# A hashed-attention and gated feed-forward block on one core: LayerNorm's factor in single columns on ScalarE, and another opening

## Chip, core and metric

The kernel runs on one core of a Trainium2 chip. The metric is the device time of one launch in microseconds (us). TensorE is called PE, VectorE DVE, ScalarE ACT, GpSimd POOL, and SyncE SP; SP's instructions are nearly all DMA issues.

## What is computed

The input x is 16 batches of 512 rows of 128 numbers. Each batch goes through attention over 16 heads of 8 numbers and then through a feed-forward net with ternary weights, both with LayerNorm before and after and a residual sum.

```python
def attn(x):                                  # x is already layer-normed
    q = (x @ Wq.T + bq).reshape(B, S, H, Dh)  # B 16, S 512, H 16, Dh 8
    v = (x @ Wv.T + bv).reshape(B, S, H, Dh)
    # six hash bits per row and head from q and hyperplanes: a bucket
    scores = einsum('bshd,bthd->bhst', q, q) / sqrt(128)
    coeff = 62 + (bucket[s] == bucket[t])
    return softmax(scores * coeff) @ v
def ffn(x):                                   # lin(x, w, s) = (x @ w.T) * s
    h = silu(lin(x, w1, s1)) * lin(x, w2, s2)            # 128 -> 512
    h = gelu(lin(h, h1, sh1)); h = gelu(lin(h, h2, sh2)) # 512 -> 512, twice
    return lin(h, w3, s3)                                # 512 -> 128
x = x + ln(attn(ln(x)));  x = x + ln(ffn(ln(x)))
```

`ln` subtracts the mean of a row and divides by the root of its variance plus 1e-5.

## The kernel before, in words

**One head.** A head's 512 x 512 scores are four tiles of 128 x 512. q is split into three bfloat16 parts, written to DRAM (`qd`, L619 and L620) and read back per head as two stacked operands `ql` (L779) and `qr` (L792); `bb` (L805) is the head's row of buckets, spread over all partitions. PE makes a score tile `sp` with one bfloat16 product (L827). DVE makes the coefficient tile `co` (L845: equal buckets, plus 62) and multiplies it with the scores into the logits `l`, taking the row maxima into `mxpad` in the same instruction (L874). The row maxima of two heads (`MH`) are turned by DVE (`mt`, L903), written to DRAM (`md`, L908) and read back once per head, spread over all partitions (`mb`, L920). Because the scores are symmetric, the maximum of a row can be subtracted along the free dimension: POOL subtracts `mb` from a whole head (L927), ACT takes the exponential (L932), and PE multiplies with v (`av`, L953), four heads into one bank, eight instructions for each of four steps. DVE divides (L984, L985).

**One batch.** `prep` normalizes x (the sums of later batches are made in `inputs`, in three groups), turns it on PE (L482), makes q (`qp`, L603), then on ACT q in float32 (`qs`, L625) and the first bfloat16 part (L708), on DVE and ACT the two others (L714, L718, L723), the bits (`pp`, L635, and L647) and buckets (L657 to L678), and v (`vp`, L741). `residual` norms the attention's result, adds x, and norms again (`norm_transposed`); `ffn` runs two gated products (`w`, L1066; silu at L1052), two hidden layers (`hp`, L1100; gelu at L1113) and the last product (`yp`, L1132), norms, adds and writes out. A float32 product with 512 columns is two PE instructions in the profile.

**LayerNorm.** `moments` (L378) leaves mean and variance of four row groups in columns. ACT adds epsilon (`ve`, L439), POOL raises to the power -1/2 (`rs`, L443), and DVE makes `nm` = -mean x rs in four instructions of one column each (`negate`, L448). `rescale` on ACT (L466) uses nm as bias and rs as scale. The letter after the underscore tells which: a for the input of batch 0, o for the attention's result, f for the net's input, y for its result.

**Weights.** `weights` (L1166) loads the five matrices and their scales, spread over all partitions, from SP's queue (L1185, L1186); POOL multiplies the scales into all five (L1189). h2 and w3 wait until the third head is gathered (`LATER`). The nets wait for all (`loaded`).

**What sets the order.** The order of instructions on every engine is fixed when the kernel is built. `Order` is a small planner: each step is a generator that asks for buffers (`get`), events (`wait`) or a turn on an engine with a cost in us and a rank; when an engine is free, the ready step with the lowest rank is emitted. On ACT the rank is a due time: the time at which the step became ready plus its rank, plus `SWITCH` if it needs another activation table. DMAs are steps of SP; the planner adds each DMA's size to one queue that drains at `DMA_RATE` = 160 KB per us (L180), and a step that holds for its data goes on `DMA_LAT` = 2.6 us after the queue has drained past it. On the chip each engine then executes its list strictly in this order and waits where data are not there. Score and net products share PE: scores have rank 0, attention products 1, preparation 2, the net 4. Buffers bound how far engines run ahead: 11 logit tiles (`LB`), 4 sets of gathered rows, 3 `mb`, 2 `mxpad`, 8 PSUM banks (3 for scores, 3 for the net, 2 for the rest).

Of the kernel before, what the change touches and what calls it, by code (L numbers as in the profile page):

```python
# [21 lines left out]
P = 128  # L22
# [24 lines left out]
class Order:  # L47
# [62 lines left out]
    def _step(self, p, value):  # L110
        while True:
            self.current = p
            try:
                want = p.gen.send(value)
            except StopIteration:
                self.live -= 1
                return
            value = None
            if want[0] == "get":
                pool = want[1]  # L120
                if not pool.free:
                    pool.waiters.append(p)
                    return
                value, deps = pool.free.pop(0)
                self._merge(p, deps)
            elif want[0] == "wait":
                if want[1].deps is None:
                    want[1].waiters.append(p)
                    return
                self._merge(p, want[1].deps)  # L130
            else:
                eng = want[1]
                when = max(
                    [self.now] + [
                        t + (self.LAT if e != eng else 0.0 if e in ("PE", "SP") else self.OWN)
                        for e, t in p.deps.items()
                    ]
                )
                self._at(when, self._offer, p, want, when)
                return  # L140
# [47 lines left out]
def tile_lsh_attention_ffn(  # L188
# [35 lines left out]
    ROOT = float(np.float32(E**-0.5))  # L224
    GROUPS = (1, 2, 6, B)
    LATE = 20
    EARLY, LATER = 2, 3
    SCALE = 1.0 / math.sqrt(E)
    AHEAD = 1
    MH = 2  # L230
# [41 lines left out]
    nc.gpsimd.memset(eps3, EPS / E**3)  # L272

    junk = const.tile([P, E], BF16, name="junk")
    warm = const.tile([P, 1], F32, name="warm")
    nc.scalar.activation(warm, eps, AF.Exp)

# [68 lines left out]
    def wait(event):  # L346
        return ("wait", event)
# [30 lines left out]
    def moments(src, name, rank, copy=None):  # L378
# [64 lines left out]
        yield pool(1.0, 0, lambda: nc.gpsimd.tensor_tensor(rs, ve, mhalf[:, 0], op=ALU.pow))  # L443

        def negate():

            for t in range(NT):
                nc.vector.tensor_scalar(  # L448
                    nm[:, t : t + 1],
                    mean[:, t : t + 1],  # L450
                    sign,
                    rs[:, t : t + 1],
                    op0=ALU.mult,
                    op1=ALU.mult,
                )

        yield dve(0.28, rank, negate)
        return nm, rs

    def rescale(src, dst, scales):  # L460
# [114 lines left out]
    def prep(b):  # L575
# [46 lines left out]
            yield dma(256, 1, emit, cost=0.7)  # L622
            od.set(kept[i])

        yield act(0.65, -2, lambda: nc.scalar.activation(qs, qp, AF.Identity, bias=bq_sb))  # L625
        read = Event()

        def buckets():
            yield wait(read)
# [73 lines left out]

        wrote, columned = Event(), Event()
        od.spawn(buckets())
        od.set(read)
        yield act(
            0.65, -2, lambda: nc.scalar.activation(qparts[0], qp, AF.Identity, bias=bq_sb)  # L708
        )
        od.spawn(keep(0))  # L710
        yield dve(
            0.63,
            1,
# [54 lines left out]
    def gather(j, tag):  # L768
        b, h = divmod(j, H)
        yield wait(prepared[b])  # L770
        ql = p1.tile([KS, S], BF16, tag=f"ql{tag}", name=f"ql_{j}")
        qr = p1.tile([KS, S], BF16, tag=f"qr{tag}", name=f"qr_{j}")
        bb = p1.tile([P, BR * BP], BF16, tag=f"bb{tag}", name=f"bb_{j}")
        rows[j] = (ql, qr, bb, tag)

        yield dma(
            74,
            1 + j * 1e-3,
            lambda: nc.sync.dma_start(  # L779
                out=ql,  # L780
                in_=qds[b][1][h]
                .rearrange("i d s -> (i d) s")
                .unsqueeze(1)
                .to_broadcast([NP * DH, NP, S]),
            ),
            held=False,
            cost=0.75,
        )
        yield dma(
            74,  # L790
            1 + j * 1e-3,
            lambda: nc.sync.dma_start(  # L792
                out=qr,
                in_=qds[b][0][h]
                .rearrange("d j s -> (d j) s")
                .unsqueeze(0)
                .to_broadcast([NP, NP * DH, S]),
            ),
            held=False,
            cost=0.72,  # L800
        )
# [57 lines left out]
    def logits():  # L859
        for j in range(B * H):  # L860
            kl = yield get(logit_bufs)
            if j % MH == 0:
                km, pair = (yield get(mx_bufs)), []
                mx = mxpads[int(km[2:])]
            l = p1.tile([P, NT, S], F32, tag=kl, name=f"l_{j}")
            base = j % MH * NT
            for t in range(NT):
                i = j * NT + t
                yield wait(scored[i])
                yield wait(weighed[i])  # L870
# [13 lines left out]

                yield dve(0.61, 5, emit)
                od.put(score_banks, ks)
                od.put(co_bufs, kc)
                if t < NT - 1:
                    od.loose()
            od.put(row_bufs, rows.pop(j)[3])  # L890
            ls[j] = (l, kl)
            pair.append((j, l))
            if len(pair) == MH:
                od.spawn(maxima(pair, mx, km))
            if j % GH == GH - 1:
                od.spawn(attend(j // GH))
            od.loose()
# [123 lines left out]
    def ffn(b, x1, k1, xnt, kx):  # L1021
        if b:
            yield wait(stages[b - 1][AHEAD])
        yield wait(loaded)
        kh = yield get(h_bufs)
        h = p1.tile([P, NC, S], F32, tag=kh, name=f"h_{b}_0")
        there = events(NC)
# [14 lines left out]
        def silus(c0, gates, half, held):  # L1042
# [5 lines left out]
            ]  # L1048

            def emit():  # L1050
                for a, (_, gp) in zip(tiles, gates):
# [32 lines left out]
        for layer in (1, 2):  # L1084
# [5 lines left out]
            for c0 in range(0, NC, 2):  # L1090
# [16 lines left out]
                        )  # L1107
                    got.append((c, kb, hp))

                def gelus(got=got, h=h, there=there):  # L1110
# [54 lines left out]

    def weights():  # L1166

        kl = yield get(logit_bufs)
        scales = p1.tile([P, NT, S], F32, tag=kl, name="scales")
        scale3 = const.tile([P, E], F32, name="scale3")  # L1170
        folded = []
        for i, (src, scale, nk, n, name) in enumerate((
            (w1_t, w1_s, 1, HID, "w1"),
            (w2_t, w2_s, 1, HID, "w2"),
            (h1_t, h1_s, NC, HID, "h1"),
            (h2_t, h2_s, NC, HID, "h2"),
            (w3_t, w3_s, NC, E, "w3"),
        )):
            w_sb[name] = w = const.tile([P, nk, n], F32, name=name)
            sc = scales[:, i, 0:n] if i < NT else scale3  # L1180
            folded.append(Event())

            def fetch(w=w, sc=sc, src=src, scale=scale, nk=nk):
                for i in range(nk):
                    nc.sync.dma_start(out=w[:, i, :], in_=src[i * P : (i + 1) * P, :])  # L1185
                nc.sync.dma_start(out=sc, in_=scale.partition_broadcast(P))  # L1186

            def fold(w=w, sc=sc, nk=nk, n=n):
                nc.gpsimd.tensor_tensor(  # L1189
                    w, w, sc.unsqueeze(1).to_broadcast([P, nk, n]), op=ALU.mult  # L1190
                )

            def piece(fetch=fetch, fold=fold, nk=nk, n=n, done=folded[-1], i=i):
                if i > EARLY:
                    yield wait(gathered[LATER])
                yield dma(nk * n / 2 + n / 2, 3, fetch, cost=0.42 * (nk + 1))
                yield pool(nk * n / 450, 2, fold)
                od.set(done)

            od.spawn(piece())  # L1200
        for e in folded:
            yield wait(e)
        od.put(logit_bufs, kl)
        od.set(loaded)

    with tc.manual_schedule():
        for piece in (prep(0), gathers(), scores(), coeffs(), logits(), weights(), inputs()):
            od.spawn(piece)
        od.run()

# [51 lines left out]
```

## Time and profile before

| | |
|---|---|
| time, median of 3 runs | 1388.59 us (1387.49, 1388.59, 1397.21) |
| profiled execution, its own time | 1398.15 us |
| its span | 1396.3 us |
| mean granted PE clock | 0.947 |
| busy PE, DVE, ACT, POOL | 1287.3, 1235.2, 1110.4, 1227.3 us |
| POOL's subtractions (L927) | 256, 4552 ns each, 1156.3 us |
| logits (L874), coefficients (L845) on DVE | 1024 each, 666.2 and 454.9 us |
| net's hidden products (L1100) on PE | 1024 instructions, 495.5 us |
| ACT: exponentials (L932), table loads | 256, 486.5 us; 176, 1283 ns each |
| DVE's `nm` (L448), groups o, f, y | 64 each, 9.2 us each |

Busy time of a group is the time that at least one of its instructions ran, so overlapping instructions count once. A line of a group reads: line, engine, operation, output <- inputs, shapes, count | busy us, mean ns of one | idle time of the engine in front of them, and what ended it. In the timeline view a line is the start in us, the length in us, the engine (SPq and ACTq are the queues that issue DMAs), and the same names; in brackets stands the idle time ahead of it. The page's slices cut the span into 40 parts of 34.9 us, with the busy share of each in tenths, and under PEclk the share of full clock that PE was granted.

### The profile page before, as it was taken

Reading aid. Unit: us, or ns where it says so; the run is one execution under the profiler, and the core shown is the slowest. Engines: PE = TensorE matmul, PEld = TensorE weight load, DVE = VectorE, ACT = ScalarE, POOL = GpSimd, SP = SyncE. Lnnn points to the kernel's source line nnn. Section 1 sums busy time; section 2 is a strip of 40 time slices with the busy share of each in tenths; the row PEclk is TensorE's granted clock in tenths of the full one; section 3 lists DMA queues with packets and bytes.
Section 4 is the critical chain, followed back from the end, with each engine's and each line's share of the span. In section 5 each row is a group of like instructions: output and inputs, shape, how many; then the busy total and the mean of one; then the engine's idle time right before and its main releaser. Section 6 shows DMA issues by size and latency. Waiting matters only on the chain.

```text
span 1396.3 us, 20309 instructions
## 1 busy us (share of the span) xinstructions
PE 1287.3 (92%) x5520; PEld 521.9 (37%) x5520; DVE 1235.2 (88%) x3985; ACT 1110.4 (80%) x1608; POOL 1227.3 (88%) x322
## 2 busy tenths in 40 slices
PE   4677699899899999999999999999999999999997
PEld 1111133434344343433444334434343344433353
DVE  5978899899899999999999999999999999999220
ACT  3566789889879888988989888888888897878752
POOL 2699799989999998999999999998999899999700
PEclk9666699899999999999999999999999999999999
DMA  5655355455445445444445544454544544444100
GB/s 172 188 132 157 103 149 149 120 144 140 122 112 151 119 131 144 123 142 120 148 122 133 148 122 140 128 136 127 142 126 132 136 135 134 127 112 116 46 8 8
DMA packets 158418, 176.09 MB, mean 126 GB/s; under 512 B 32480, under 2 KB 115680, under 8 KB 158304
## 3 DMA queue, kind: packets, MB, share of 16 engines
q1 hardware_dynamic: 157872, 174.59, 45.6%
q8 instruction: 44, 0.72, 0.2%
q14 instruction: 70, 0.57, 0.2%
q10 hardware_dynamic: 432, 0.20, 0.0%
HBM read 155.59 MB, written 19.14 MB: 125 GB/s over the span
## 4 chain that ended last, share of the span: by engine, by line
PE 63%; DVE 21%; issue 6%; DMA 4%; POOL 3%; ACT 2%; SPq 0%; POOLq 0%; DVEq 0%
PE hp L1100 24%; PE av L953 16%; PE sp L827 12%; DVE l L874 10%; DVE co L845 7%; PE w L1066 3%; PE yp L1132 3%; POOL l L927 2%; DMA mb<-md 2%; PE op L974 1%; PE pp L635 1%; PE qp L603 1%; DMA ql<-qd 1%; PE vp L741 1%; ACT l L932 1%
## 5 line engine op out<-in xcount | busy, mean ns | idle before, releaser
L927 POOL TENSOR_TENSOR l<-l,mb 128x2048 f32<-128x2048 f32 x256 | 1156.3, 4552 | 36.4 <-DMA mb<-md 32.0
L874 DVE CUSTOM_DVE_ANT_0 l<-co,sp 128x512 f32<-128x512 bf16 x1024 | 666.2, 686 | 29.2 <-PE av L953 22.3
L932 ACT ACTIVATE l<-l 128x2048 f32<-128x2048 f32 x256 | 486.5, 1907 | 41.2 <-POOL l L927 40.0
L1100 PE MATMUL hp<-h,h 128*128 128x512 f32 x1024 | 495.5, 596 | 0.2 <-ACT h L1113 0.2
L845 DVE TENSOR_SCALAR co<-bb,bj 128x516 bf16<-128x516 bf16 x1024 | 454.9, 477 | 3.9 <-DMA bb<-bkd 3.8
L827 PE MATMUL sp<-qr,ql 72*128 72x512 bf16 x1024 | 378.3, 404 | 80.6 <-DVE mxpad L874 68.3
L953 PE MATMUL av<-l,vaug 128*32 128x512 f32 x2048 | 280.7, 636 | 0.4 <-DVE y L1156 0.2
L1100 PEld LDWEIGHTS hp<-h,h 128*128 128x128 f32 x1024 | 190.5, 190 | 176.0 <-issue 152.9
L827 PEld LDWEIGHTS <-ql 72*128 72x128 bf16 x1024 | 96.7, 99 | 410.6 <-issue 383.4
L1066 PE MATMUL w<-xnt_f,w 128*128 128x512 f32 x256 | 133.0, 616 | 3.2 <-ACT y L390 2.0
L932 ACT ACT_TABLE_LOAD x86 | 110.3, 1283 | 1.5
L967 ACT COPY avs<-av 128x512 f32<-128x512 f32 x64 | 37.3, 582 | 90.1 <-PE av L953 90.1
L1113 ACT ACTIVATE h<-hp 128x512 f32<-128x512 f32 x128 | 71.0, 595 | 33.9 <-PE hp L1100 33.3
L953 PEld LDWEIGHTS av<-l,vaug 128*32 128x32 f32 x2048 | 47.8, 112 | 123.0 <-issue 89.9
L874 DVE DVE_READ_ACCUMULATOR2_ANT mxpad<- 128x1 f32 x1024 | 91.6, 89 | 0.0
L1113 ACT ACT_TABLE_LOAD x58 | 74.4, 1283 | 0.8
L1132 PEld LDWEIGHTS yp<-w,h 128*128 128x128 f32 x512 | 67.0, 196 | 12.7 <-issue 8.1
L1036 DVE TENSOR_TENSOR h<-w,a 128x512 f32<-128x512 f32 x64 | 43.9, 687 | 27.8 <-PE w L1066 22.0
L1132 PE MATMUL yp<-w,h 128*128 128x128 f32 x512 | 67.9, 280 | 0.0
L1066 PEld LDWEIGHTS w<-xnt_f,w 128*128 128x128 f32 x256 | 47.6, 196 | 50.9 <-issue 21.5
L443 POOL TENSOR_TENSOR rs_y<-ve_y,mhalf 128x4 f32<-128x4 f32 x16 | 16.2, 1010 | 51.8 <-issue 34.7
L448 DVE TENSOR_SCALAR nm_y<-su_y,rs_y 128x1 f32<-128x1 f32 x64 | 9.2, 210 | 38.5 <-POOL rs_y L443 38.5
(91 smaller groups left out, 868.8 us busy)
## 6 DMA issues: line engine op xcount, KB each, us to landing
mb<-md SPq DMA_DIRECT2D x256, 256.0 KB
bb<-bkd SPq DMA_DIRECT2D x256, 130.5 KB
ql<-qd SPq DMA_DIRECT2D x256, 72.0 KB
qr<-qd SPq DMA_DIRECT2D x256, 72.0 KB
qd<-q SPq DMA_DIRECT2D x96, 128.0 KB
xta<-in_L_attn_x_dram SPq DMA_DIRECT2D x16, 256.0 KB
xtr<-in_L_attn_x_dram SPq DMA_DIRECT2D x16, 256.0 KB
out_dram<-y SPq DMA_DIRECT2D x16, 256.0 KB
```

What stands on the lines that cost most here:

```text
L827: nc.tensor.matmul(sp, lhsT=ql[:, ts(t, P)], rhs=qr, start=True, stop=True)
L845: nc.vector.tensor_scalar(co, bb.rearrange("p (r c) -> p r c", c=BP)[:, :, 0:BC], bjs[b][:, c : c + 1], float(NBKT - 2), op0=ALU.is_equal, ...
L874: nc.vector.tensor_tensor_reduce(out=l, in0=co[:, 0:S], in1=sp, scale=1.0, scalar=-3.0e38, op0=ALU.mult, op1=ALU.max, accum_out=mx[:, t : ...
L927: lambda: nc.gpsimd.tensor_tensor(l, l, mb.unsqueeze(1).to_broadcast([P, NT, S]), op=ALU.subtract),
L932: yield act(1.82, 0, lambda: nc.scalar.activation(l, l, AF.Exp, scale=SCALE), "exp")
L953: nc.tensor.matmul(av[k * Q : (k + 1) * Q, :], lhsT=va[:, t, c : c + Q], rhs=ls[gg * GH + k][0][:, t, :], start=(t == 0), stop=(t == NT - 1),)
L967: yield act(0.5, -2, lambda: nc.scalar.copy(avs, av))
L1036: lambda: nc.vector.tensor_tensor(h[:, c, :], g2, a, op=ALU.mult),
L1066: lambda: nc.tensor.matmul(gp, lhsT=w_sb[which][:, 0, ts(c, P)], rhs=xnt, start=True, stop=True),
L1100: lambda i=i: nc.tensor.matmul(hp, lhsT=w[:, i, ts(c, P)], rhs=hin[:, i, :], start=(i == 0), stop=(i == NC - 1),),
L1113: nc.scalar.activation(h[:, c, :], hp, AF.Gelu)
L1132: nc.tensor.matmul(yp[:, ts(t, E)], lhsT=h[:, i, ts(t, P)], rhs=w_sb["w3"][:, i, :], start=(i == 0), stop=(i == NC - 1),)
```

## The change

`negate` moves to ACT: `mm` = sign x mean is made ahead of the power, and four ACT copies of one column each multiply it with rs. The scales of w1, h1 and h2 are no longer multiplied into the weights but given as per-partition scale columns to the silu and gelu activations; those of w2 and w3 still are. The weights are issued from ACT's queue as ACT steps with rank `LATE` (20), one after another, w2 and w3 first, h2 after the first head is gathered; only three small scale columns go by SP. PE gets `activity`, products of a zero tile (128 x 512, bfloat16) with rank 99, planned at 0.45 us each up to 10 us and at 0.25 us afterwards, until the first net is `started`. For batch 0, `qs` is made by DVE beside ACT's first part. The first head's `qr` is issued from ACT's queue. The maxima of the first four heads (`SINGLES`) are sent head by head.

```diff
@@ Order._step
+            elif want[0] == "rest":
+                self._at(self.now + want[1], self._step, p, None)
+                return
@@
-    EARLY, LATER = 2, 3
+    COLD = 10.0
+    SINGLES = 4
@@
+    still = const.tile([P, P], BF16, name="still")
+    nc.vector.memset(still, 0.0)
+    started = []
@@ moments
+        mm = p2.tile([P, NT], F32, tag=f"mm{q}", name=f"mm_{name}")
+
+        def negate():
+            for t in range(NT):
+                nc.scalar.activation(
+                    nm[:, t : t + 1], mm[:, t : t + 1], AF.Copy, scale=rs[:, t : t + 1]
+                )
+
+        yield act(0.22, -5, lambda: nc.scalar.activation(mm, mean, AF.Copy, scale=sign))
         yield pool(1.0, 0, lambda: nc.gpsimd.tensor_tensor(rs, ve, mhalf[:, 0], op=ALU.pow))
-
-        def negate():
-
-            for t in range(NT):
-                nc.vector.tensor_scalar(
-                    nm[:, t : t + 1],
-                    mean[:, t : t + 1],
-                    sign,
-                    rs[:, t : t + 1],
-                    op0=ALU.mult,
-                    op1=ALU.mult,
-                )
-
-        yield dve(0.28, rank, negate)
+        yield act(0.8, -4, negate)
@@ prep
-        yield act(0.65, -2, lambda: nc.scalar.activation(qs, qp, AF.Identity, bias=bq_sb))
         read = Event()
+
+        def copied():
+            yield dve(
+                0.66,
+                1,
+                lambda: nc.vector.tensor_scalar(qs, qp, bq_sb, None, op0=ALU.add),
+            )
+            od.set(read)
@@
-        od.set(read)
+        if b:
+            yield act(0.65, -2, lambda: nc.scalar.activation(qs, qp, AF.Identity, bias=bq_sb))
+            od.set(read)
+        else:
+            od.spawn(copied())
         yield act(
             0.65, -2, lambda: nc.scalar.activation(qparts[0], qp, AF.Identity, bias=bq_sb)
         )
         od.spawn(keep(0))
+        yield wait(read)
@@ gather
+        queue = nc.sync if j else nc.scalar
...
-            lambda: nc.sync.dma_start(
+            lambda: queue.dma_start(
                 out=qr,
...
-            cost=0.72,
+            cost=0.72 if j else 0.05,
@@ logits
-            if j % MH == 0:
+            if j < SINGLES or j % MH == 0:
                 km, pair = (yield get(mx_bufs)), []
...
-            base = j % MH * NT
+            base = len(pair) * NT
...
-            if len(pair) == MH:
+            if j < SINGLES or len(pair) == MH:
                 od.spawn(maxima(pair, mx, km))
@@ ffn
         yield wait(loaded)
+        started.append(b)
...
-                    nc.scalar.activation(a, gp, AF.Silu)
+                    nc.scalar.activation(a, gp, AF.Silu, scale=w_sb["w1s"][:, c : c + 1])
...
-                            nc.scalar.activation(h[:, c, :], hp, AF.Gelu)
+                            nc.scalar.activation(
+                                h[:, c, :], hp, AF.Gelu, scale=sc[:, c : c + 1]
+                            )
@@ weights (new body)
+        for layer, (src, scale, nk, n, name) in enumerate((
+            (w2_t, w2_s, 1, HID, "w2"),
+            (w3_t, w3_s, NC, E, "w3"),
             (w1_t, w1_s, 1, HID, "w1"),
             (h1_t, h1_s, NC, HID, "h1"),
             (h2_t, h2_s, NC, HID, "h2"),
         )):
             w_sb[name] = w = const.tile([P, nk, n], F32, name=name)
+            if layer == 4:
+                yield wait(gathered[0])
+            for i in range(nk):
+                yield act(
+                    0.42,
+                    LATE,
+                    lambda: nc.scalar.dma_start(out=w[:, i, :], in_=src[i * P : (i + 1) * P, :]),
+                )
+            if name in ("w2", "w3"):
...
+                yield act(
+                    0.42,
+                    LATE,
+                    lambda: nc.scalar.dma_start(out=sc, in_=scale.partition_broadcast(P)),
+                )
+                yield ("rest", 6.0)
+                yield pool(
+                    nk * n / 420,
+                    2,
+                    lambda: nc.gpsimd.tensor_tensor(
+                        w, w, sc.unsqueeze(1).to_broadcast([P, nk, n]), op=ALU.mult
+                    ),
+                )
...
+            else:
+                w_sb[name + "s"] = sc = const.tile([P, NC], F32, name=name + "s")
+                yield dma(
+                    2,
+                    2,
+                    lambda: nc.sync.dma_start(
+                        out=sc,
+                        in_=scale.rearrange("(c p) -> p c", p=P),
+                        allow_slow_non_contiguous=True,
+                    ),
+                    cost=0.6,
+                )
         od.set(loaded)
@@ new
+    def activity():
+        kb = yield get(ffn_banks)
+        bk = bank(kb, "activity")
+
+        def emit(start=False, stop=False):
+            nc.tensor.matmul(
+                bk,
+                lhsT=still,
+                rhs=still.unsqueeze(1).to_broadcast([P, NT, P]),
+                start=start,
+                stop=stop,
+            )
+
+        yield pe(0.45, 99, lambda: emit(start=True))
+        while not started:
+            yield pe(0.45 if od.now < COLD else 0.25, 99, emit)
+        yield pe(0.25, 99, lambda: emit(stop=True))
+        od.put(ffn_banks, kb)
```

`activity` is started last, beside the other generators.

More of the change, by code (lines that the diff above doesn't have):

```diff
@@ L442, in moments @@
         )
[L443 removed]
+        mm = p2.tile([P, NT], F32, tag=f"mm{q}", name=f"mm_{name}")
         def negate():
             for t in range(NT):
[L448 to L457 removed]
+                nc.scalar.activation(
+                    nm[:, t : t + 1], mm[:, t : t + 1], AF.Copy, scale=rs[:, t : t + 1]
+                )
+        yield act(0.22, -5, lambda: nc.scalar.activation(mm, mean, AF.Copy, scale=sign))
+        yield pool(1.0, 0, lambda: nc.gpsimd.tensor_tensor(rs, ve, mhalf[:, 0], op=ALU.pow))
+        yield act(0.8, -4, negate)
         return nm, rs
@@ L1050, in emit @@
             def emit():
-                for a, (_, gp) in zip(tiles, gates):
-                    nc.scalar.activation(a, gp, AF.Silu)
+                for i, (a, (_, gp)) in enumerate(zip(tiles, gates)):
+                    c = c0 + i
+                    nc.scalar.activation(a, gp, AF.Silu, scale=w_sb["w1s"][:, c : c + 1])
             yield act(1.2, 0, emit, "silu")
@@ L1108, in ffn, with gelus @@
                     got.append((c, kb, hp))
-                def gelus(got=got, h=h, there=there):
+                def gelus(got=got, h=h, there=there, sc=w_sb[f"h{layer}s"]):
                     def emit():
                         for c, _, hp in got:
-                            nc.scalar.activation(h[:, c, :], hp, AF.Gelu)
+                            nc.scalar.activation(
+                                h[:, c, :], hp, AF.Gelu, scale=sc[:, c : c + 1]
+                            )
                     yield act(1.2, 0, emit, "gelu")
@@ L1166, in weights @@
     def weights():
[L1168 to L1172, printed above, removed]
+        for layer, (src, scale, nk, n, name) in enumerate((
+            (w2_t, w2_s, 1, HID, "w2"),
+            (w3_t, w3_s, NC, E, "w3"),
             (w1_t, w1_s, 1, HID, "w1"),
-            (w2_t, w2_s, 1, HID, "w2"),
             (h1_t, h1_s, NC, HID, "h1"),
@@ L1176, in weights @@
             (h2_t, h2_s, NC, HID, "h2"),
-            (w3_t, w3_s, NC, E, "w3"),
         )):
             w_sb[name] = w = const.tile([P, nk, n], F32, name=name)
[L1180 to L1186, printed above, removed]
@@ L1188, in fold @@
-            def fold(w=w, sc=sc, nk=nk, n=n):
-                nc.gpsimd.tensor_tensor(
-                    w, w, sc.unsqueeze(1).to_broadcast([P, nk, n]), op=ALU.mult
-                )
[L1193 to L1203, printed above, removed]
-        od.set(loaded)
+            if layer == 4:
[5 more added lines that the diff above has]
+                    lambda: nc.scalar.dma_start(out=w[:, i, :], in_=src[i * P : (i + 1) * P, :]),
+                )
+            if name in ("w2", "w3"):
+                if name == "w2":
+                    kl = yield get(logit_bufs)
+                    sc = p1.tile([P, NT, S], F32, tag=kl, name="scale2")[:, 0, :]
+                else:
+                    sc = const.tile([P, E], F32, name="scale3")
+                yield act(
[11 more added lines that the diff above has]
+                )
+                if name == "w2":
+                    od.put(logit_bufs, kl)
+            else:
+                w_sb[name + "s"] = sc = const.tile([P, NC], F32, name=name + "s")
[9 more added lines that the diff above has]
+                )
@@ L1206, in tile_lsh_attention_ffn @@
     with tc.manual_schedule():
-        for piece in (prep(0), gathers(), scores(), coeffs(), logits(), weights(), inputs()):
+        for piece in (prep(0), gathers(), scores(), coeffs(), logits(), weights(), inputs(), activity()):
             od.spawn(piece)
```

## The prediction

> **What bounds the kernel now.** I read the slices of the span first, then busy time by stretch, then GpSimd's instructions in order of time, then SyncE's at the opening, then the chain that ended last.
>
> Slices: GpSimd (POOL) has an empty opening, a long full stretch and an empty tail, and the granted clock is low in slices 2 to 5.
>
> ```profile
> POOL 2699799989999998999999999998999899999700
> PEclk9666699899999999999999999999999999999999
> ```
>
> Busy time by stretch (columns: length, then PE, PEld, DVE, ACT, POOL busy, then clock, DMA share, GB/s). Up to 175 us PE has half or three quarters of its clock. From 250 to 1300 us, fourteen such stretches add up to 1016 us of PE, 1008 of DVE, 1002 of POOL and 895 of ACT in 1050: three engines at 95 to 97%, ACT at 85%.
>
> ```profile
> 57.00:75.00 18.00, 11.65 (x24) 1.85 (x23) 16.68 (x52) 11.05 (x21) 18.00 (x5) 0.50 0.70 165
> 150.00:175.00 25.00, 19.14 (x60) 4.88 (x59) 20.50 (x74) 16.33 (x33) 17.97 (x6) 0.58 0.41 106
> 625.00:700.00 75.00, 73.97 (x331) 30.62 (x329) 74.00 (x240) 65.23 (x84) 71.13 (x19) 1.00 0.48 137
> ```
>
> POOL's instructions in order of time: the softmax subtraction (L927), 256 times 4.52 us, first runs at 52.37 us; the last ends at 1317.6, and 78.7 us follow. From 52 us on POOL hardly rests; one hole of 7.03 us is at 155, where the first feed-forward LayerNorm's power waits for ScalarE, and ScalarE (ve_f at 161.86) stood behind a copy that waited for the av products, 1.87 us per block of eight there and 1.00 later.
>
> ```profile
> 39.86 4.51 POOL L1189 TENSOR_TENSOR h<-h,scales 128x2048 f32<-128x2048 f32 x1 [20.93 <-DMA w<-in_L_ffn_w_w_dram]
> 52.37 35.97 POOL L927 TENSOR_TENSOR l<-l,mb 128x2048 f32<-128x2048 f32 x8 [6.78 <-DMA mb<-md]
> 162.23 1.01 POOL L443 TENSOR_TENSOR rs_f<-ve_f,mhalf 128x4 f32<-128x4 f32 x1 [7.03 <-ACT ve_f L439]
> ...
> 1308.60 9.01 POOL L927 TENSOR_TENSOR l<-l,mb 128x2048 f32<-128x2048 f32 x2
> ```
>
> SyncE's queue at the opening: the first maxima are written (md) at 34.85 and read back (mb) only at 48.10, though the transfer between is 16 KB. SP issues in order; the planner counts every SP transfer into one queue of 160 KB/us (L180), so the weights' 1.6 MB (h2, w3 and their scales) put the planned landing of md some 10 us back, and other issues in front of mb.
>
> ```profile
> 34.85 0.56 SPq L908 DMA_DIRECT2D md<-mt  x1
> 37.74 2.31 SPq L1185 DMA_DIRECT2D w<-in_L_ffn_w_w_dram  x4
> 46.34 0.56 SPq L908 DMA_DIRECT2D md<-mt  x1
> 48.10 1.09 SPq L920 DMA_DIRECT2D mb<-md  x2
> ```
>
> The chain says what holds the long stretch: PE and DVE in turn.
>
> ```profile
> PE 63%; DVE 21%; issue 6%; DMA 4%; POOL 3%; ACT 2%; SPq 0%; POOLq 0%; DVEq 0%
> ```
>
> So the time is: when the subtractions start, how fast four nearly full engines pass 256 heads, and a tail.
>
> **The change, part by part.** The profiled execution took 1398.15 us (span 1396.3, 1.85 around it), 9.56 above the median 1388.59; the runs lie near 1388 and near 1397, and no view tells me why. I work out a difference, and set it against the median.
>
> *Opening, A.* The first coefficient (L845) runs at 24.57. Four edits move it. qs goes to DVE beside q0 on ACT: one ACT instruction of 0.68 leaves the line, -0.68. qp on a warmed PE: its pair took 2.07, a warm pair of the same shape (hp) 1.02, -1.05. nm_a on ACT: four columns of 0.84 in front of the scaling where DVE's first was ready after 0.28, +0.6. The first qr from ACT's queue: bb is issued 0.82 earlier (20.41 to 21.23). Sum -1.9: 22.7. Head 0's last logits ended at 29.42; alone, its maxima are turned (0.21) at 29.63 - 1.9 = 27.7, where the pair's were at 33.92. md is issued 0.93 later as before, 28.65. The gap md to mb is unknown: 13.25 and 9.74 (46.34 to 56.08) with weights in the planner's queue, 3.2 (62.70 to 65.90) without. In the new plan the weights are on ACT's queue and not counted, but the first gathers are; I take 6, nearer the last row. mb lands 4.27 after its issue (48.10 to 52.37): first subtraction at 38.9, 13.4 earlier. Pairs begin again at head 4: five more heads at 4.0 of DVE and 2.4 of the second batch's preparation put head 5's last logits at 49.9, and its mb at 61.3; POOL is ready at 38.9 + 4 x 4.52 = 57.0 and waits 4.3, where it waited 0.9 before. A = -13.4 + 3.4 = **-10**; with a gap of 3.2 it is -12.8, with 9.74 -6.3, with 13.25 -2.8.
>
> What pays for this: SP loses 19 weight and scale issues (9.4 us by its rows) and gets 3 scale columns (0.6 each by hb_sb's row) and 2 more md (0.56). ACT gets 16 weight issues of 0.43 and one qr of 0.75, 7.6 us, in a queue busy 21.5 of the first 57 us; behind a qr that waits for qd stand only sums of later batches and weights. Two more transposes cost DVE 0.4. I put +1 (0 to 5) for data that now collide with the first gathers. The folds of w1, h1, h2 leave POOL (1.27 + 2 x 4.5); they lay before 52.37, so they are worth nothing in themselves, but with POOL starting at 38.9 the h2 fold at 39.86 would have cost its 4.5.
>
> The skill's page "DMA: Bandwidth & Descriptors" (Issuing engines are not separate DMA queues) speaks against expecting much here: issuing from several engines saves only issue time, since the same 16 DMA engines move the data. By it alone the move would be worth the 0.82 and the SP issues in front of mb, 2.7, not the rest; I go by the order of SP's queue, which the rows show.
>
> *Opening, B.* Zero products fill PE's planned gaps until the first feed-forward starts, one every 0.25 us by plan, a warm 512-column bf16 product (sp) taking 0.215 in a row. If they hold the clock, av's blocks before 172 us take 1.00 for 1.87 and the 7.03 hole closes: **-7**, ends 0 (clock not held) and -10 (four slow blocks of group 4, 3.5, as well). A filler in front of a real product costs at most 0.25 and is gone before the long stretch.
>
> *LayerNorm's factor, C.* 48 LayerNorms later than the opening lose four DVE instructions each: three groups of 9.2 busy us.
>
> ```profile
> L448 DVE TENSOR_SCALAR nm_f<-mv_f,rs_f 128x1 f32<-128x1 f32 x64 | 9.2, 212 | 2.8 <-POOL rs_f L443 2.8
> L439 ACT ACTIVATE ve_f<-mv_f,eps 128x4 f32<-128x4 f32 x16 | 4.7, 294 | 6.4 <-DVE mv_f L427 6.4
> L625 ACT ACTIVATE qs<-qp,bq_sb 128x512 f32<-128x512 f32 x16 | 10.9, 680 | 7.4 <-PE qp L603 7.4
> ```
>
> Of 27.6 us, 6.9 lie on the chain (nm_f 4.31, nm_o 1.39, nm_y 1.22, added over its pieces). I take **-6.9**. Above: nothing, if PE alone sets the pace; below: -24, the part between 250 and 1300, if DVE does (PE rests 34 us there).
>
> *ACT, D.* Five small activations per LayerNorm instead. The trace has none with one column and a scale column. Bounds: 0.165 (mp, no pointer) and 0.294 (ve, bias column) each, 40 to 71 us over 48; scaling pairs show instructions of 0.485 that follow each other after 0.38, so four cost about 0.294 + 3 x 0.18 = 0.84, with mm 1.0, 48 us in all. Silu and gelu get a scale column: 0.68 (L625) against 0.595 (gelu), 192 x 0.085 = 16. ACT: +64. Cover: 155 us of ACT's rest between 250 and 1300, and only 2% of the chain is ACT's; without it all 64 show. The negation now waits for POOL's power at ACT's head, with exps and gelus behind it, where DVE stood 6.3 us up to 1310. In the tail nothing covers three LayerNorms at 0.55 more: **+1.8** with the last gelus.
>
> The skill's page "ScalarE: Activation LUTs" (Rules for kernel authors) says adds and multiplies belong on VectorE. By its figures (186 ns, 93 per pointer column, 93 of overlap; section What ACT_TABLE_LOAD costs) four columns are an estimated 0.84, DVE's four span 0.58 here: by the rule alone the move is a loss of 0.26 each, 12 us, by the chain a gain, because DVE is on it.
>
> Sum: -10 - 7 - 6.9 + 1.8 + 1 = **-21.1**. Against the profiled execution 1377.05, against the median **1367.5**.
>
> **The rivals.** *R1, DVE sets the pace.* For it: DVE at 96%, and after 57 us it rests mostly on PE. Against: PE has 63% of the chain. C is -24: 1350.4. *R2, POOL's early start is given back*: SP's order still holds mb back, or DVE falls behind. A is -3: 1374.5. *R3, ACT becomes the bound, slower.* Place: exps behind a negation that waits for POOL, so av frees logit buffers late (DVE waited 22.3 us for av already). Against: ACT rests 15%. If two thirds of its 64 us show, +42.7: 1410.2. It decides from a third (21.1 of 64); 55% make it over 1% slower. *R4, the fillers do not hold the clock*: B is 0 and qp stays cold: 1375.6.
>
> **How the numbers follow.** Forecast 0.50 (own range 1355 to 1380), R1 0.15, R2 0.15, R3 0.12, R4 0.08. 1% is 13.9 us, about what a measurement of this kernel can tell from no change: 1374.7 and 1402.5. Faster: 0.42 of the forecast, 0.15, 0.08 of R2, 0.03 of R4, 0.68. Slower: 0.09 of R3. Same: 0.23. The range goes from 1343 (R1 with A at -12.8 and B at -10 is 1344.6) to 1394 (A -3, B 0, C 0, +5 for the transfers and D's +1.8 give 1392.4), leaving out most of R3 and a little of R1, under 0.2.
>
> **What would show it.** A: the first L927 near 39 (R2: past 48), mb 3 to 10 us after the first md. B: a granted clock near 1.0 from 57 to 175, av blocks of 1.0, no 7 us hole before the first rs_f. C: no L448-like group on DVE, DVE's busy time near 1207, PE's rest from 250 to 1300 below 34. D: ACT near 1175 us busy, exps not waiting longer than now; R3 would show as DVE waiting for av far above 22 us. Wrong altogether, if the last subtraction ends less than 10 us earlier although the first starts 13 earlier.

## The result and the profile after

The changed kernel ("after") takes 1386.23 us (median of 17 runs, 1382.42 to 1390.08), the kernel before 1393.01 in its 17 runs on the same chips (1387.49 to 1397.21): a ratio of 0.995, 95% interval 0.9937 to 0.9963. It is a gain of 7 us where 21 were forecast. The profiled execution of after took 1382.42 us (span 1380.6) and is the shortest of its runs; that of before, 1398.15, is longer than all its 17. So 9 of the 15.7 us between the two traces are only the choice of execution.

The slices of after, GpSimd and the granted clock:

```profile
POOL 1599999999999999999999999989999999999200
PEclk9999999999999999999999999999999999999998
```

The low clock of slices 2 to 5 is gone, and so is GpSimd's dip to 7 in slice 5; its first two slices are no fuller than before. By stretch (length, then PE, PEld, DVE, ACT, POOL busy, clock, DMA share, GB/s), the same three stretches:

```profile
57.00:75.00 18.00, 17.97 (x89) 7.79 (x91) 17.90 (x56) 8.39 (x21) 10.63 (x4) 1.00 0.62 164
150.00:175.00 25.00, 24.87 (x131) 9.29 (x130) 23.44 (x77) 18.43 (x39) 25.00 (x8) 1.00 0.48 143
625.00:700.00 75.00, 74.68 (x344) 31.61 (x343) 73.75 (x231) 70.52 (x103) 74.73 (x20) 1.00 0.50 137
```

The clock is 1.00 for 0.50 and 0.58 (PE's busy time there now includes zero products), but from 57 to 75 us POOL is busy 10.63 of 18 us where it was busy throughout. ACT went from 65.23 to 70.52 of 75 us in the third. GpSimd's instructions in order of time:

```profile
41.17 4.53 POOL L943 TENSOR_TENSOR l<-l,mb 128x2048 f32<-128x2048 f32 x1 [20.89 <-DMA mb<-md]
48.81 9.03 POOL L943 TENSOR_TENSOR l<-l,mb 128x2048 f32<-128x2048 f32 x2 [3.11 <-DMA mb<-md]
63.82 4.53 POOL L943 TENSOR_TENSOR l<-l,mb 128x2048 f32<-128x2048 f32 x1 [5.98 <-DMA mb<-md]
69.74 22.56 POOL L943 TENSOR_TENSOR l<-l,mb 128x2048 f32<-128x2048 f32 x5 [1.39 <-DMA mb<-md]
...
159.21 1.00 POOL L459 TENSOR_TENSOR rs_f<-ve_f,mhalf 128x4 f32<-128x4 f32 x1
```

The first subtraction starts 11.2 us earlier, then POOL waits 3.11, 5.98 and 1.39 us for maxima. Its sixteenth subtraction ends at 126.7; before's ended at 127.1 (91.12 + 8 x 4.5). The hole before the first rs_f is closed. The last subtraction ends at 1283.9 for 1317.6, but 96.7 us follow for 78.7, with 128 of the nets' hidden products where before's tail had 115.

ACT's new and widened instructions, and the chain:

```profile
L1070 ACT ACTIVATE a<-w,w1s 128x512 f32<-128x512 f32 x64 | 40.9, 684 | 1.6 <-PE w L1084 0.9 <-DVE mv_o L434 0.2
L454 ACT ACTIVATE nm_y<-mm_y,rs_y 128x1 f32<-128x1 f32 x64 | 13.5, 283 | 3.0 <-POOL rs_y L459 3.0
L458 ACT ACTIVATE mm_y<-su_y 128x4 f32<-128x4 f32 x16 | 3.1, 195 | 0.0
```

```profile
PE 68%; DVE 17%; DMA 5%; ACT 4%; issue 3%; POOL 2%; SPq 1%; POOLq 0%; DVEq 0%; ACTq 0%
```

DVE lost 4 points of the chain, PE won 5, ACT rose from 2% to 4%.

### The profile page after: what moved, and what is told of

Its sections match the earlier page's. It is cut to its first block, busy times and chain, and to the rows that moved or that the text cites. A ratio compares the mean times of both kernels' runs of the same rounds, so it can differ in the third digit from the quotient of the medians.

```text
span 1380.6 us, 21164 instructions
## 1 busy us (share of the span) xinstructions
PE 1323.2 (96%) x5929; PEld 550.7 (40%) x5929; DVE 1213.3 (88%) x3793; ACT 1162.0 (84%) x1851; POOL 1217.0 (88%) x319
## 4 chain that ended last, share of the span: by engine, by line
PE 68%; DVE 17%; DMA 5%; ACT 4%; issue 3%; POOL 2%; SPq 1%; POOLq 0%; DVEq 0%; ACTq 0%
PE hp L1118 25%; PE av L969 16%; PE sp L843 13%; DVE l L890 8%; DVE co L861 5%; PE w L1084 4%; PE yp L1152 3%; PE activity L1247 3%; POOL l L943 2%; DMA mb<-md 2%; DMA bb<-bkd 1%; PE op L990 1%; ACT l L948 1%; PE vp L756 1%; DMA qr<-qd 1%
## 5 line engine op out<-in xcount | busy, mean ns | idle before, releaser
L890 DVE CUSTOM_DVE_ANT_0 l<-co,sp 128x512 f32<-128x512 bf16 x1024 | 664.6, 681 | 25.7 <-PE av L969 17.6
L861 DVE TENSOR_SCALAR co<-bb,bj 128x516 bf16<-128x516 bf16 x1024 | 449.7, 472 | 5.1 <-DMA bb<-bkd 4.9
L843 PE MATMUL sp<-qr,ql 72*128 72x512 bf16 x1024 | 356.4, 382 | 33.2 <-DVE mxpad L890 31.2
L969 PE MATMUL av<-l,vaug 128*32 128x512 f32 x2048 | 270.0, 611 | 0.0
L1247 PE MATMUL activity<-still 128*128 128x512 bf16 x409 | 109.4, 391 | 1.0 <-DVE still L280 1.0
L890 DVE DVE_READ_ACCUMULATOR2_ANT mxpad<- 128x1 f32 x1024 | 85.5, 84 | 0.0
L1247 PEld LDWEIGHTS <-still 128*128 128x128 bf16 x409 | 40.2, 100 | 58.3 <-issue 20.1
```

Source lines behind the costliest of these rows:

```text
L843: nc.tensor.matmul(sp, lhsT=ql[:, ts(t, P)], rhs=qr, start=True, stop=True)
L861: nc.vector.tensor_scalar(co, bb.rearrange("p (r c) -> p r c", c=BP)[:, :, 0:BC], bjs[b][:, c : c + 1], float(NBKT - 2), op0=ALU.is_equal, ...
L890: nc.vector.tensor_tensor_reduce(out=l, in0=co[:, 0:S], in1=sp, scale=1.0, scalar=-3.0e38, op0=ALU.mult, op1=ALU.max, accum_out=mx[:, t : ...
L969: nc.tensor.matmul(av[k * Q : (k + 1) * Q, :], lhsT=va[:, t, c : c + Q], rhs=ls[gg * GH + k][0][:, t, :], start=(t == 0), stop=(t == NT - 1),)
L1247: nc.tensor.matmul(bk, lhsT=still, rhs=still.unsqueeze(1).to_broadcast([P, NT, P]), start=start, stop=stop,)
```

## The experiments

At first I held that PE was the bound (96% busy), so that relieving DVE and adding to ACT were both worth little. Rivals: ACT's added work costs what the rest gains; the opening's gain is eaten by weight transfers. Times below are medians, with the ratio to before in brackets.

### Four undoings

**e1**: after, with the factor back on DVE.

```diff
-        yield act(0.22, -5, lambda: nc.scalar.activation(mm, mean, AF.Copy, scale=sign))
         yield pool(1.0, 0, lambda: nc.gpsimd.tensor_tensor(rs, ve, mhalf[:, 0], op=ALU.pow))
-        yield act(0.8, -4, negate)
+        yield dve(0.28, rank, negate)   # negate as in before
```

> The changed kernel with LayerNorm's factor back on DVE, all else kept (DVE +28 us of work, ACT -48). Theory PE (from the first net product on, PE's whole remaining work sets the end, and an earlier end of the attention only leaves more net products for the tail): the last subtraction ends 8 to 25 us later than the changed kernel's 1283.9, the tail is shorter by as much, and the time stays within 4 us of the changed kernel's 1386. Rival ACT (the added ACT work gave the gain back): about 20 us faster, 1366. Rival DVE (DVE sets the pace): 15 to 25 us slower, over 1400.

1371.30 us (0.9849, 0.9817 to 0.9882), nearest to the rival ACT. Giving the factor back to DVE gained 15 us on after, in this order.

**e2**: after, the weights on ACT's queue held back further.

```diff
-            if layer == 4:
-                yield wait(gathered[0])
+            if layer in (1, 3, 4):
+                yield wait(gathered[{1: 1, 3: 3, 4: 5}[layer]])
```

> The changed kernel with the loads of w3, h1 and h2 put off until the second, fourth and sixth head is gathered, so that they do not share the DMA engines with q's writes and the first gathers. Theory that these transfers cost the opening: the first coefficient comes at 23 to 24.5 us instead of 27.6, the first subtraction at 35 to 38 instead of 41.2, the first net product up to 5 us earlier than 173.4, and the time falls by what the first net product gains, 0 to 5 us. Rival (the transfers are hidden, the wait has another cause): first coefficient still past 27, time the same within 2.

1399.88 (1.0043, 1.0022 to 1.0064). The first coefficient comes at 24.76 (after 27.63), the first subtraction at 38.17 (41.17), the first product of a feed-forward net at 166.78 (173.35): so the weights do delay the opening. Yet the kernel is 14 us longer, outside theory and rival: the last subtraction ends at 1290.1 and 105 us follow.

**e3**: after without `activity()`.

```diff
-        for piece in (..., weights(), inputs(), activity()):
+        for piece in (..., weights(), inputs()):
```

> The changed kernel without the zero products. Theory PE: granted clock 0.5 to 0.8 again between 57 and 175 us, a hole of some us before the first feed-forward LayerNorm's power, first net product 3 to 10 us later than 173.4, time later by the same, 1389 to 1396. Rival (the clock of the opening is hidden behind the subtractions): time within 2 us of 1386.

1385.36 (0.9944, 0.9925 to 0.9963). Without the zero products the clock from 57 to 175 us is 0.66, where after has 1.00 (e3, then after):

```profile
57.00:175.00 118.00, 84.56 (x310) 21.46 (x310) 106.91 (x339) 75.42 (x164) 107.58 (x27) 0.66 0.52 144
57.00:175.00 118.00, 117.38 (x614) 45.43 (x613) 113.64 (x360) 77.93 (x161) 110.63 (x28) 1.00 0.54 152
```

The first net starts 9.8 us later, and the time is the same. Ten microseconds at the start were not ten at the end. But an edit also moves the planned order: DVE's sequence leaves that of after at 43 us in e2 and e3 and at 252 us in e4, so each of these three runs is one order against another.

**e4**: after, with a quarter of the second hidden layer's products left out, 55 us of PE's work.

```diff
-                    for i in range(NC):
+                    for i in range(NC if layer == 1 else NC - 1):
...
```

> The changed kernel with a quarter of the second hidden layer left out (three of four input chunks): PE loses 128 instructions of 0.43 us, 55 us, and no other engine loses anything. Theory PE: 35 to 55 us faster, 1331 to 1351, with the tail after the last subtraction shorter by most of it (97 us now). Rivals ACT and DVE: PE's work is not what sets the end, under 10 us.

1382.90 (0.993, 0.9906 to 0.9955), only 3 us below after, where my first theory said 35 to 55: PE's total work alone doesn't set the time. Stretches from the first net's start to the last subtraction's end, after and then e4:

```profile
173.35:1283.90 1110.55, 1072.93 (x4826) 442.24 (x4822) 1055.79 (x3298) 1008.96 (x1482) 1084.86 (x273) 0.99 0.48 133
```

```profile
176.27:1303.20 1126.93, 1062.24 (x4758) 432.93 (x4754) 1058.46 (x3300) 1017.10 (x1507) 1086.29 (x274) 0.97 0.47 131
```

With less to do PE rests 64.7 us instead of 37.6, at a clock of 0.97 instead of 0.99: two points of 1127 us, an estimated 23 us more. By that estimate the lost clock took nearly as much as the 27 us of longer rests. The Trainium skill's page "Perfetto Trace Analysis" (Identifying the Most-Contended Engine) takes the engine with the highest occupancy for the one to relieve first, with a caution that PE's busy share is no measure of headroom; e4 fits the caution: at 96% busy, 55 us less of PE's work took 3 us off, in this one order.

### ACT's load, and the order

e1 left two readings: ACT's added work costs time, or the hand-written planner merely fell into a luckier order. Each changed cost makes the planner choose another order for all that follows. So e5 adds work to ACT on which nothing waits, e6 does the factor's move alone, and e7 and e8 keep every instruction of after and change one planned cost by about 1% or less.

**e5**: e1 with five one-column activations per LayerNorm, written to a tile that nobody reads.

```diff
+    slack = const.tile([P, 8], F32, name="slack")
+    def ballast(src):
+        od.loose()
+        def emit():
+            for t in range(NT + 1):
+                nc.scalar.activation(slack[:, t : t + 1], eps, AF.Copy, scale=eps)
+        yield act(1.02, 3, emit)
@@ moments
+        if name[0] != "a":
+            od.spawn(ballast(src))
```

> e1 (factor on DVE) with the same five small ScalarE instructions per LayerNorm as the changed kernel's, but writing a tile that nobody reads: ACT gets the added 48 us of work, DVE keeps its factor, and nothing waits for the new instructions. Theory load (ScalarE's added work itself costs the 15 us between e1's 1371 and the changed kernel's 1386): 1383 to 1400. Rival latency (the cost is that LayerNorm's chain now passes ScalarE's queue once more): within 4 us of e1, 1367 to 1375.

**e6**: before, with the factor moved to ACT and nothing else.

> The kernel before with LayerNorm's factor on ACT alone, the opening and the scales as before. Theory that the factor on ACT costs about 15 us on either side: 1400 to 1412 against 1394 of the kernel before. The forecast's own step (6.9 us off the chain): 1385 to 1390. Rival that the cost of the factor in e1 against the changed kernel was only another order of the same instructions: anything, 1380 to 1410, without relation to 15.

**e7** and **e8**: after, in another order.

```diff
-        yield dve(0.45, 1, divide)          # e7
+        yield dve(0.455, 1, divide)
-        yield act(1.82, 0, ... AF.Exp ...)  # e8
+        yield act(1.815, 0, ... AF.Exp ...)
```

> The changed kernel with one planned cost changed, the division's, from 0.45 to 0.455 us: the same instructions, in another order. Theory order (the planner's greedy order is unstable now that four engines are nearly full, and a difference of ten microseconds between two kernels can be the order alone): 10 to 20 us faster than the changed kernel's 1386, as the planner's own clock stops 21.5 us earlier. Rival (orders differ little): 1384 to 1389.

> The changed kernel with the exponential's planned cost changed from 1.82 to 1.815 us: the same instructions, in another order. Theory order: 10 to 28 us slower than the changed kernel's 1386, as the planner's own clock stops 27.5 us later. Rival (orders differ little): 1384 to 1389.

e5 1408.33 (1.0089, 1.0056 to 1.0121), above its theory's 1400; e6 1385.65 (0.9923, 0.9898 to 0.9948); e7 1368.41 (0.9803, 0.9774 to 0.9832); e8 1415.38 (1.0136, 1.0109 to 1.0163). The same instructions in two orders differ by 47 us, seven times the result, so no single comparison of two orders says what a part of the change is worth. e5 stands 37 us above e1. Its load is this, for the whole execution (ACT's busy time grew by 42.7 us, 1127.7 to 1170.4, as small neighbours overlap):

```profile
L391 ACT ACTIVATE slack<-eps 128x1 f32<-128x1 f32 x240 | 49.2, 281 | 0.0
```

Where it shows are three waits of the loop over heads: logits that wait for a buffer which av frees (DVE l <- PE av), score products that wait for logits to leave their bank (PE sp <- DVE mxpad), subtractions that wait for maxima (POOL l <- DMA mb). The waits from 250 to 1260 us (total, times, longest), for before, after, e1, e5, e7 and e8 in turn:

```profile
POOL l L927 <- DMA mb<-md: 25.3, 15, 4.8
PE sp L827 <- DVE mxpad L874: 24.6, 54, 2.8
...
DVE l L874 <- PE av L953: 9.3, 9, 2.2
```

```profile
PE sp L843 <- DVE mxpad L890: 28.2, 59, 1.5
...
DVE l L890 <- PE av L969: 13.7, 10, 3.1
...
POOL l L943 <- DMA mb<-md: 6.7, 4, 1.9
```

```profile
PE sp L846 <- DVE mxpad L893: 18.8, 40, 2.0
...
POOL l L946 <- DMA mb<-md: 9.6, 8, 2.2
...
DVE l L893 <- PE av L972: 5.9, 3, 2.3
```

```profile
POOL l L958 <- DMA mb<-md: 32.6, 13, 8.7
PE sp L858 <- DVE mxpad L905: 29.5, 60, 1.7
DVE l L905 <- PE av L984: 21.6, 10, 4.2
```

```profile
PE sp L843 <- DVE mxpad L890: 17.4, 43, 1.5
...
DVE l L890 <- PE av L969: 6.9, 5, 2.2
POOL l L943 <- DMA mb<-md: 3.3, 2, 2.0
```

```profile
PE sp L843 <- DVE mxpad L890: 40.5, 69, 2.3
DVE l L890 <- PE av L969: 26.2, 15, 5.4
POOL l L943 <- DMA mb<-md: 21.6, 17, 3.3
```

The sums are 59, 49, 34, 84, 28 and 88 us, against profiled executions of 1398, 1382, 1370, 1406, 1364 and 1413. Over all kernels here but e4 (19) the sum and the time of the profiled execution correlate at 0.92, 0.71 us of time per us of wait, with misses up to 13 us. The waits go with the time; that they are its cause isn't shown by a correlation, and the three were picked with the traces at hand. e4 has less work than the others; its waits, 91 us, are the largest of all, and the fit would put its profiled execution at 1414 where it took 1387. So less work on PE may have been worth more than e4's 3 us, behind a poorer order. In e5 no instruction reads what the added work writes, and ACT still rests 112 us of these 1010, yet the logit buffers come back later (21.6 for 5.9). The same 1010 us in e1 and then e5:

```profile
250.00:1260.00 1010.00, 978.17 (x4434) 405.57 (x4433) 993.20 (x3206) 891.83 (x1162) 986.99 (x249) 0.99 0.48 134
250.00:1260.00 1010.00, 967.03 (x4305) 405.63 (x4303) 956.52 (x3073) 898.26 (x1327) 946.28 (x240) 0.98 0.46 130
```

### The same parts in several orders

To tell a part from an order, e9 to e14 put the edits of e7 and e8 on the other three combinations of factor and opening; e15 and e16 move a third planned cost of after by 2% either way.

```diff
e9  = e1 + divide 0.455        e10 = e1 + exp 1.815
e11 = before + divide 0.455    e12 = before + exp 1.815
e13 = e6 + divide 0.455        e14 = e6 + exp 1.815
e15 = after, avs copy 0.49 for 0.50    e16 = after, avs copy 0.51
```

> e1 (the changed kernel with the factor on DVE) in another order: the division planned at 0.455 us for 0.45, as in e7. Theory (with the factor on DVE the order is stable, and the factor on ACT costs some 15 us in the mean over orders): 1366 to 1376, near e1's 1371. Rival (e1 was a lucky order, and the factor's place is worth nothing in the mean): scattered as the changed kernel's three orders are, 1368 to 1415.

> e1 in a third order: the exponential planned at 1.815 us for 1.82, as in e8. Theory: 1366 to 1378. Rival: scattered over 1368 to 1415.

> The kernel before in another order: the division planned at 0.455 us. Theory (the kernel before has its factor on DVE too and is as stable as e1): 1388 to 1402 around its 1395. Rival (its 1395 was luck as well): below 1380 or above 1405.

> The kernel before in a third order: the exponential planned at 1.815 us. Theory: 1388 to 1402. Rival: below 1380 or above 1405.

> e6 (the kernel before with the factor on ACT alone) in another order: division planned at 0.455 us. Theory (ACT's added work costs some 15 us in the mean and makes the order unstable; e6's 1386 was a lucky order): 1398 to 1412. Rival (the factor alone is a gain with the old opening, as forecast): 1380 to 1392.

> e6 in a third order: exponential planned at 1.815 us. Theory: 1400 to 1418. Rival: 1380 to 1392.

> The changed kernel in a fourth order, picked by a rule and not by its outcome: the copy of the attention product planned at 0.49 us for 0.50. Theory order (scatter of tens of us around a mean near 1390): somewhere in 1370 to 1410, the planner's own clock says 2.3 us under the changed kernel's. Rival (the scatter was only e7's and e8's): 1384 to 1389, which this run alone can't tell apart from the theory.

> The changed kernel in a fifth order, by the same rule: that copy planned at 0.51 us. Theory order: 1395 to 1410, as the planner's clock stops 15.6 us later than the changed kernel's. Rival: 1384 to 1389.

Medians in us; the ratio, with its interval, is to before's runs on the same chip, and before's median lies between 1393.01 and 1397.51 from chip to chip:

| planned cost | old opening, factor DVE | old opening, factor ACT | new opening, factor DVE | new opening, factor ACT |
|---|---|---|---|---|
| as written | before 1393.01 | e6 1385.65 | e1 1371.30 | after 1386.23 |
| divide 0.455 | e11 1396.51 (1.0028, 1.0007 to 1.0048) | e13 1404.40 (1.0048, 1.0032 to 1.0064) | e9 1378.23 (0.9897, 0.9849 to 0.9945) | e7 1368.41 |
| exp 1.815 | e12 1383.78 (0.9927, 0.9906 to 0.9948) | e14 1410.74 (1.0092, 1.0065 to 1.012) | e10 1372.02 (0.9855, 0.9806 to 0.9903) | e8 1415.38 |
| mean | 1391.1 | 1400.3 | 1373.9 | 1390.0 |

e15 took 1387.93 (0.9917, 0.989 to 0.9944), e16 1407.95 (1.0065, 1.0045 to 1.0085). e7 and e8 were picked as extremes by the planner's own count, so the last column's spread is wider than a draw would give; after, e15 and e16, not picked, have a mean of 1394.0. e9 lies 2 us above its theory's range and e12 between theory and rival; the other six lie in their theory's range, e15 in its rival's as well.

With the factor on DVE the new opening is worth -21.7, -18.3 and -11.8 us in the three orders: one sign, mean -17. With the factor on ACT it is +0.6, -36.0 and +4.6. The factor's move to ACT makes -7.4, +7.9, +27.0 in the old opening and +14.9, -9.8, +43.4 in the new: mean +12.7, both signs, a standard error of 8.3 over the six, so not clear of zero. Taken against before on each run's own chip, the six have a mean of +10, and e6 alone is -10.4. e12, ten microseconds below before on its chip, shows that before's own order costs that much.

### A better order, and the load again

**e17**: e1 without the zero products, with six single heads and other planned costs, picked as the order that the planner's own count put earliest.

```diff
-    LAT = 0.3
+    LAT = 0.28
-    SINGLES = 4
+    SINGLES = 6
-        yield act(1.82, 0, ... AF.Exp ...)
+        yield act(1.85, 0, ... AF.Exp ...)
-        yield act(0.5, -2, lambda: nc.scalar.copy(avs, av))
+        yield act(0.55, -2, lambda: nc.scalar.copy(avs, av))
```

> A version meant to be the fastest: the factor on DVE, the new opening without the zero products, the first six maxima single, and the planned costs of the exponential (1.85), the copy of the attention product (0.55) and the hand-over between engines (0.28) set so that the planner's own clock stops earliest, out of 1500 sets tried. Theory (the planner's clock ranks orders): 1356 to 1368, under every other run. Rival (its small differences mean nothing on the chip): 1368 to 1380, as e1's orders.

**e18**: e5 with the divide planned at 0.455.

> e5 (factor on DVE, and the same five small ACT instructions per LayerNorm without a reader) in another order: division planned at 0.455 us. Theory load (ACT's added work itself costs 15 us or more, whatever waits for it): 1385 to 1412. Rival (e5's 1408 was an unlucky order): 1368 to 1380.

e17 1379.11 (0.9893, 0.9867 to 0.9918): shorter than both kernels, not than e1, e7, e9 or e10. The planner's own clock, at the end of the build, says 1361.1 for e17 and misses it by 18 us; it doesn't find the best order. For the other 19 kernels it is within 12 us of the median, and it has most of the load's price: 1374.2 for e1 and 1405.2 for e5, 1371.4 for e9 and 1404.9 for e18. For before it says 1384.6 and for after 1386.9, so it had no gain in the change before anything ran. e18 1410.59 (1.0119, 1.0085 to 1.0153), 32 us above e9. So the load on ACT costs 37 and 32 us in two pairs (35 and 31 against before on the same chip), where the e1 family (e1, e9, e10) spreads over 7: more than the luck of an order there. The load moves the order too (DVE's sequence in e5 leaves that of e1 at 151 us), so this is its price together with the order that the planner makes around it; no run separates the two.

## Why the prediction was wrong, step by step

**What bounds the kernel.** I read four nearly full engines that pass heads to each other, and that reading stands. What failed is what I did with it: I added up terms of one order's chain as if the others stayed put. e3, e2 and e4 show it, each in one order: 9.8 us later, 6.6 us earlier and 55 us less work came out as -1, +14 and -3.

**D, "Cover: 155 us of ACT's rest", is the step that failed.** It let 64 us of ACT's work show as 1.8. The sizes of the instructions were right: four columns take 0.84 in a row (0.84 said), factor and mm 50 us by their groups (48 said), silu and gelu 0.685 for 0.595; ACT's busy time as a whole rose by 51.6 (1110.4 to 1162.0), not 64, as neighbours overlap. The cover was wrong. 49 us of small ACT work that nothing reads cost 37 and 32 us (e5, e18). In the order as written, e1 to after, the factor's move is +14.9 where I had summed -6.9 and most of +1.8; all the rest of the change, silu's and gelu's columns with it, is -21.7 (before to e1), where I had -10, -7 and +1. In that order the whole miss sits here. Over six pairs the move costs 13 +- 8, less than the load alone. The 2% that ACT held of the chain was no evidence of cover: with the load ACT holds 3% (e5) and 5% (e18). The third that I set as the point of decision for R3 was passed by e5's load, though not by the change as a whole, and R3's sign stayed silent: DVE waited 17.6 us for av in after, where I looked for far above 22. The Trainium skill's rule that adds and multiplies belong on VectorE ("ScalarE: Activation LUTs", Rules for kernel authors), which I set against the chain, has the sign of the mean on its side, as far as 13 +- 8 has one; its reason, time per element, has little to do with instructions of one element per partition (283 ns each here).

**C, -6.9 from DVE's share of the chain.** e6 alone would have confirmed it (-7.4, or -10.4 on its own chip). In the other two orders of the same opening it is +7.9 and +27.0. But these numbers hold D's cost as well. With about the same small work on ACT, the factor on DVE (e5, e18) takes 22 and 42 us more than the factor on ACT (after, e7). By these pairs DVE's relief is worth more than 6.9, about R1's 24 or above, and ACT's load takes more than that away. The orders differ in each pair, and e7 was picked for its order, so the size stays open, and R1, DVE sets the pace, is not refuted.

**A, -10.** The opening's first step was nearly as said: -11.2 for -13.4 at the first subtraction, and the gap from md to mb was 3.7 (33.87 to 37.55) where I took 6. The rest of the step was not. I had the maxima of heads 1 to 3 ready when POOL is; POOL waited 3.1 us for head 1's and 6.0 for head 3's. The first coefficient came 3.1 later instead of 1.9 earlier:

```profile
27.63 1.65 DVE L861 TENSOR_SCALAR co<-bb,bj 128x516 bf16<-128x516 bf16 x4 [4.10 <-DMA bb<-bkd]
```

The coefficient started 5.0 after bb's issue, for 3.3 before, with h1's loads on ACT's queue beside it; and q0 on ACT waited for qs on DVE, where I had them side by side:

```profile
13.80 0.69 ACT L722 ACTIVATE q<-qp,bq_sb 128x512 bf16<-128x512 f32 x1 [0.75 <-DVE qs L634]
```

POOL then starved for 10.5 us instead of 4.3, and by its sixteenth subtraction the lead was 0.4. This is R2's outcome, the lead given back, with DVE behind as R2 had it, here for want of bb. With the loads held back (e2) the sixteenth ends at 122.1, a lead of 5.0. Yet e2 takes longer, and the new opening as a whole is worth 17 us with the factor on DVE. So its worth doesn't come by the path I worked out. Which part pays it, the folds gone from GpSimd, the moved issues or the single maxima, no run here separates; the fillers alone changed nothing (e3, in one order).

**B, -7.** Every sign came true: clock 1.00, qp's warm pair at 1.13, the hole closed, R4 refuted. In the time it came out as nothing (e3), though with another order on either side.

**The net.** The tail's +1.8 was 18: attention ended 33.7 us earlier and the nets' products moved behind it. My sign for being wrong altogether, a last subtraction less than 10 us earlier, therefore stayed silent. The end of one stage can't serve as a sign where another stage's work can slide behind it.

**What stays open.** Why 49 us of unawaited ACT work cost 35 with 112 of rest left: that exps and gelus come a little later, and av with them, fits DVE's wait for av (5.9 to 21.6), but I only argue it. The planner's clock, in which every instruction has a fixed cost, has 31 and 34 of it, so turns, waits and order may be enough. Why the shuffled orders differ is shown as waits, not traced to a first cause.

## What to carry to other kernels

Where four engines are each over 85% full and run one fixed order, an engine's rest is not cover: price added work on the engine that takes it by loading it there with work that nobody reads. Where the order is planned by a program, measure each variant in several orders, by nudging one planned cost, before a difference below the spread is put down to the edit. Read loop waits for buffers across variants; the chain's shares did not follow the time (PE 72% in e7 and 67% in e14, which are 42 us apart, and 47% in e1, 3 us from e7). A planner's own clock is worth reading before the run: here it had after no faster than before.

## What the runs showed of the hardware

With zero products of 128 x 512 bfloat16 the granted clock was 1.00 from 57 to 175 us (after) where it was 0.66 without them (e3). A stretch in which PE was 94% busy (e4) had a clock of 0.97, one of 97% (after) 0.99; that loss, an estimated 23 us, was nearly as large as the added rest (27 us). One activation with a scale column instead of a constant takes 0.684 for 0.595 us at 128 x 512 (after and before).
